# One residual-norm layer of a four-layer mix: its inverse root moved between engines, its scaling spread out, and two reorderings in the LSTM around it

## The chip, the cores and the metric

The kernel runs on one NeuronCore of a Trainium2 chip. Its engines work side by side, each with an instruction queue in order: TensorE (PE, matmuls; PEld are its weight loads), VectorE (DVE), ScalarE (ACT), GpSimd (POOL) and SyncE (SP), which here only issues DMAs. The metric is the time of one execution in microseconds (us), and lower is better. A profile shows one execution in detail; its span runs from the first instruction to the last, and the execution's own time is a little longer.

## The reference, cut to what matters

Four layers work on one tensor `x` of 128 x 64 x 256 (batch, nodes, features), each as a residual with a layer norm behind it. Layer 0 is the one that the change touches: a graph convolution, then for p = 1 to 4 an LSTM over windows of p neighbouring nodes, whose last hidden state replaces the last node of each window before the next p begins.

```python
def _L0_gnn_ref(x, adj, Wg0, bg0, Wg1, bg1, Wih, Whh, bih, bhh):
    h = relu(einsum('ts,bsh->bth', adj, x @ Wg0 + bg0))
    h = relu(einsum('ts,bsh->bth', adj, h @ Wg1 + bg1))
    for p in range(1, 5):
        nw = T // p
        wins = h[:, :nw * p, :].reshape(B * nw, p, Hd)
        last = _lstm_last(Wih[p-1], Whh[p-1], bih[p-1], bhh[p-1], wins)
        h = h.at[:, arange(nw) * p + (p - 1), :].set(last.reshape(B, nw, Hd))
    return h

def _layernorm(x, eps=1e-5):
    return (x - mean(x)) / sqrt(var(x) + eps)      # over the 256 features

x = _layernorm(x + _L0_gnn_ref(x, adj, ...))   # layer 0
x = _layernorm(x + _L1_gnn_ref(x, adj, ...))   # graph convolution, batch norms
x = _layernorm(x + _L2_gnn_ref(x, ..., adj))   # graph attention
x = _layernorm(x + _L3_gnn_ref(x, adj, ...))   # spectral: needs eigh(L_norm)
```

One LSTM step forms four gates i, f, g, o from `x_t @ Wih.T + h @ Whh.T + bias`, then `c = sig(f) * c + sig(i) * tanh(g)` and `h = sig(o) * tanh(c)`. Layer 3 needs the eigenvectors of a 64 x 64 matrix. They depend on `adj` alone, and the kernel works them out on VectorE during layer 0.

## The kernel before, in words

`x` lies in SBUF as the tile `X`: 64 tiles of 128 rows (two graphs of 64 nodes each) by 256 features. Layer 0 works on four groups of `TG` = 16 tiles (group 0 to 3). All matmuls are fp32.

**One group.** `convolve` (L1607) makes the group's hidden state `H` with features on the partitions. It is a generator, one `yield` after each small portion. `windows` (L1646) runs the LSTM of one p over the group. It splits the work into `parts`: four for p=1, two for p=2 and p=3 (one batch, that is, one graph of each tile pair, in each part), and a single one of both batches for p=4. A part has M columns: 512, or 336 for p=3. In a part, step `k` walks over the four gates `gt` (0 i, 1 f, 2 g, 3 o; f is skipped at k=0) and two feature halves `c`. One (gt, c) is one product tile in PSUM from the pool `pq`, which has four buffers: two input products (`inputs`, L1665 to L1670, reading `H` through `at`), for k>0 two recurrent ones (`recurrent`, L1672 to L1675, reading the last step's `lh`), and an eviction on ScalarE with sigmoid or tanh (L1696), which frees the buffer. For k>0 the two tiles of gate 0 are formed ahead, both inputs first and then the recurrent products (L1677 to L1682). VectorE forms the cell (L1703, L1706, L1708, L1709), ScalarE takes its tanh (L1710), VectorE multiplies by the output gate into `lh` (L1712) or, in the last step, into the places of `H` that end a window (L1717). So p=4 reads what p=3 has just written to `H`. The trace shows every fp32 matmul of the program as two records on PE, each with a weight load of its own.

**What is interleaved.** `pump` (L1699) lets the eigen solver (its pieces are lines 118 to 149 and about 800 to 880, tiny instructions on 64 partitions) go on by some instructions behind each eviction; VectorE's queue is shared by both. `side` (L1700) advances a generator by work done: `paced` (L1729) gives it `n` steps over a given amount of LSTM work. During p=3 and p=4 the side job is the next group's `convolve`. During p=1 and p=2 it is the previous group's `residual` (L1719): eight steps, each of which transposes two tiles of `H` back on PE (four transposes into the one buffer of the pool `pr`) and hands them to `ln.add`. Group 3's residual runs in the first pass of layer 1 (L1841).

**The norm.** `Norm.add` (L1273) adds the two tiles to `X` (L1279), takes the statistics of each (L1282, L1283) and after eight tiles calls `flush` (L1288). It calls `inv_sqrt` (L1251): on VectorE variance plus epsilon (L1257), on ScalarE a Sqrt (L1259), and on VectorE four more instructions that refine and invert it (L1260 to L1263). Then VectorE scales the eight tiles one behind the other (L1300). ScalarE's Sqrt needs another function table than sigmoid and tanh, which share one; a change of table is an instruction of its own, ACT_TABLE_LOAD. Layers 1 to 3 use `Norm` as well and are left as they are.

**What sets the order.** A scheduler may reorder instructions of an engine between the places where the program emits them, by dependences and pools; products marked with `keep_in_program_order` stay. SP's queue holds the weight loads of each p (`wi`, `wh`, 1 MB each), the inputs of the groups, and, from layer 1 on, copies of `X` to DRAM (`xd`).

## Time and profile before

| | us |
|---|---|
| three runs | 2254.89, 2255.51, 2256.37 |
| their median | 2255.51 |
| the profiled execution, its own time | 2254.81 |
| its span | 2253.0 |
| granted clock of PE, mean | 0.994 |
| POOL busy, of the span | 161.7 (7%) |
| idle of PE ahead of L1669 in layer 0 (77 to 1420 us) | 13.1 |
| its products there: L1669 (2010 records) and L1674 (1152 records), busy | 809.9 and 461.9 |
| evictions L1696 there (504), mean ns | 631 |

How to read it: "busy" is the time in which an engine has an instruction under way. A row of a timeline gives the start in us, the duration, the engine, the line, the operation, output and inputs by the program's names with their shapes, the number of instructions joined in it, and in brackets the idle time just before it and what ended that. A row of the waits gives who waited on which line, for whose result on which line, and the total, the number and the longest of these waits. "Slices" cut the span in 40 equal parts and give busy tenths in each. A row of the windows gives for a stretch of time its length, the busy time and the instructions of PE, PEld, DVE, ACT and POOL, and then the granted clock of PE, the share of time in which DMA is busy, and GB/s.

### The profile page before, as it was taken

How to read it: one execution, taken by the hardware profiler on the slowest of the kernel's cores; microseconds unless marked ns; L12 is line 12 of the kernel's file. 1: busy time of each engine (PE TensorE's matmuls, PEld its weight loads, DVE VectorE, ACT ScalarE, POOL GpSimd, SP SyncE). 2: the span in 40 equal slices, each digit the busy share in tenths (PEclk: the TensorE clock that was granted, in tenths of full speed). 3: DMA queues.
4: the chain of work that ended last, by engine and by line, in shares of the span. 5: the costliest groups of instructions: out<-in, count | busy, mean ns of one | idle time of the engine just before them, and what ended most of it. 6: DMA issues, size and time to landing. Idle time of an engine off the chain costs nothing. (4 is left out here: it accounts for less than half of the span.)

```text
span 2253.0 us, 29801 instructions
## 1 busy us (share of the span) xinstructions
PE 2197.9 (98%) x8746; PEld 1198.6 (53%) x8746; DVE 1808.5 (80%) x9217; ACT 952.3 (42%) x1746; POOL 161.7 (7%) x196
## 2 busy tenths in 40 slices
PE   8999999999999999999999999999999999999997
PEld 6445655445655445655444654554434333445987
DVE  5788887889888889888889998788947777657688
ACT  1432322433322343322343222434437876567675
POOL 0111111111000000000000000000000000100631
PEclk9999999999999999999999999999999999999999
DMA  7001010111010111010101000012210010221532
GB/s 233 22 19 38 1 39 1 38 38 57 1 38 1 38 38 57 1 38 1 38 38 56 1 19 19 20 54 98 74 54 24 29 42 24 77 74 43 151 90 80
DMA packets 44666, 101.53 MB, mean 45 GB/s; under 512 B 5297, under 2 KB 23857, under 8 KB 43217
## 3 DMA queue, kind: packets, MB, share of 16 engines
q1 hardware_dynamic: 38384, 84.64, 11.0%
q0 software_dynamic: 3984, 14.40, 2.3%
q8 instruction: 69, 1.13, 0.2%
q10 hardware_dynamic: 2128, 0.54, 0.1%
q14 instruction: 101, 0.82, 0.1%
HBM read 67.97 MB, written 31.59 MB: 44 GB/s over the span
## 5 line engine op out<-in xcount | busy, mean ns | idle before, releaser
L1669 PE MATMUL pq<-H,wi 128*128 128x512 f32 (+1 forms) x2016 | 812.6, 543 | 13.3 <-ACT gate L1696 7.0
L1696 ACT ACTIVATE gate<-pq,bl 128x512 f32<-128x512 f32 (+1 forms) x504 | 314.4, 631 | 610.6 <-PE pq L1674 497.8
L1669 PEld LDWEIGHTS pq<-H,wi 128*128 128x128 f32 x2016 | 377.2, 191 | 364.5 <-issue 281.1
L1674 PE MATMUL pq<-lh,wh 128*128 128x512 f32 (+1 forms) x1152 | 461.9, 528 | 0.9 <-DVE lh L1712 0.8
L1674 PEld LDWEIGHTS pq<-lh,wh 128*128 128x128 f32 x1152 | 218.1, 190 | 203.1 <-issue 144.2
L2097 DVE SCALAR_TENSOR_TENSOR xs<-xs 128x512 f32<-128x512 f32 x256 | 165.1, 685 | 70.1 <-ACT xs L2096 69.2
L1710 ACT ACTIVATE gate<-lc 128x512 f32<-128x512 f32 (+1 forms) x144 | 83.6, 580 | 276.4 <-DVE lc L1709 105.0
L2096 ACT COPY xs<-l 128x512 f32<-128x512 f32 x256 | 134.0, 596 | 53.9 <-PE l L2091 43.9
L2091 PE MATMUL l<-edge_s,xq 64*128 64x512 f32 x512 | 128.7, 616 | 0.4 <-ACT xs L2096 0.3
L2054 PE MATMUL m<-wqv,xT 128*128 128x512 f32 (+1 forms) x264 | 121.7, 597 | 2.8 <-DVE X L1279 1.9
L1913 PE MATMUL ps<-h,w 128*128 128x512 f32 x256 | 114.0, 603 | 3.2 <-ACT h L1907 3.2
L1298 ACT ACTIVATE X<-X,ln_sh,ln_rs 128x256 f32<-128x256 f32 x187 | 97.5, 592 | 40.7 <-DVE ln_sh L1294 31.2
L1860 PE MATMUL ps<-at,w 128*128 128x512 f32 x256 | 113.1, 593 | 0.0
L796 POOL PARTITION_ALL_REDUCE qQ<-qSG x62 | 73.5, 1186 | 512.6 <-DVE pc L134 291.1
L1282 DVE BATCH_NORM_STATS2 ln_st<-X 128x6 f32<-128x256 f32 x256 | 98.3, 414 | 1.5
L2054 PEld LDWEIGHTS m<-wqv,xT 128*128 128x128 f32 x264 | 46.4, 189 | 76.4 <-issue 36.1
L1913 PEld LDWEIGHTS ps<-h,w 128*128 128x128 f32 x256 | 48.6, 193 | 62.5 <-issue 53.2
L1860 PEld LDWEIGHTS ps<-at,w 128*128 128x128 f32 x256 | 47.2, 190 | 52.8 <-issue 51.9
L2091 PEld LDWEIGHTS l<-edge_s,xq 64*128 64x128 f32 x512 | 44.5, 186 | 56.9 <-issue 41.8
L1712 DVE TENSOR_TENSOR lh<-gate 128x512 f32<-128x512 f32 (+1 forms) x72 | 43.1, 602 | 33.7 <-ACT gate L1696 33.7
L130 DVE SCALAR_TENSOR_TENSOR CS<-GA,qE 64x1 f32<-64x1 f32 x294 | 61.7, 210 | 9.5
L130 DVE SCALAR_TENSOR_TENSOR GA<-qtg,CS,GA 64x1 f32<-64x1 f32 x294 | 61.6, 209 | 8.5
(611 smaller groups left out, 3277.1 us busy)
## 6 DMA issues: line engine op xcount, KB each, us to landing
wi<-in_WihT_dram SPq DMA_DIRECT2D x16, 1024.0 KB, 4.9
wh<-in_WhhT_dram SPq DMA_DIRECT2D x12, 1024.0 KB, 6.7
xd<-X SPq DMA_DIRECT2D x16, 512.0 KB, 2.6
X<-xd SPq DMA_DIRECT2D x16, 512.0 KB, 3.4
xv<-xv SPq DMA_DIRECT2D x32, 256.0 KB, 2.0
xr<-xv POOLq DMA_DIRECT2D x32, 256.0 KB, 3.0
X<-in_x_dram SPq DMA_DIRECT2D x15, 512.0 KB, 8.9
out_dram<-X SPq DMA_DIRECT2D x15, 512.0 KB, 2.9
```

Source lines behind the costliest of these rows:

```text
L130: self.nc.vector.scalar_tensor_tensor(o, a, s, b, op0, op1)
L1282: nc.vector.bn_stats(st, self.X[:, k, :])
L1298: nc.scalar.activation(x, x, AF.Identity, bias=sh[:, k : k + 1], scale=rs[:, k : k + 1])
L1669: te.matmul(ps, wi[:, kk, o * P : (o + 1) * P], at(kk, k), start=(kk == 0), stop=(k == 0 and kk == 1))
L1674: te.matmul(ahead[gt, c], wh[:, kk, o * P : (o + 1) * P], hst[:, kk, :M], start=False, stop=(kk == 1))
L1696: s.activation(gates[gt][:, c, :M], ps, AF.Tanh if gt == 2 else AF.Sigmoid, bias=bl[:, p - 1, o : o + 1])
L1860: te.matmul(ps, w1[:, k, c * P : (c + 1) * P], at[:, k, :], start=(k == 0), stop=(k == 1))
L1913: te.matmul(ys[c], w2[:, k, c * P : (c + 1) * P], h[:, k, :], start=(k == 2), stop=(k == 1))
L2054: te.matmul(pss[i][:, cols], xT[:, i, c, :], wqv[:, c, cols], start=(c == 0), stop=(c == 1))
L2091: mm = te.matmul(pl[:, b, :], xq[i][r, c * P : (c + 1) * P], GG[r, :], start=True, stop=True)
L2096: taken.setdefault(i, []).append(s.copy(x, pl[:, b, :]))
L2097: ready.append(v.scalar_tensor_tensor(x, x, 0.2, x, ALU.mult, ALU.max))
```

## The change

Four edits, all in layer 0:

1. `SpreadNorm` takes the place of `Norm`. After eight tiles it doesn't take the inverse root and scale them at once; it puts ten jobs on a list `late`: the first part of the root, the rest of it, and eight scalings of one tile each. `step(3)` does up to three of them. The root is computed on VectorE alone: a first value from the bits of the number (one multiply-add on them as integers), and three corrections, 12 instructions in all.
2. `residual` calls `ln.step(3)` ahead of each `ln.add`, and after its eight steps goes on until the list is empty. `paced` gives it `TG // 2 + 4` = 12 steps over the same amount of work instead of 8.
3. In p=4 at k=0 the four tiles of gates 0 and 2 are formed together by `by_batch`: first the columns of batch 0 of all four, then those of batch 1, in matmuls of 256 columns.
4. The cell's tanh is emitted behind the next eviction (`due`) instead of right where the cell is formed. In the built order the scheduler moves most of them back ahead of it.

```diff
+class SpreadNorm:
+    def add(self, t, src, n=1):
...
+        if len(self.todo) == self.n:
+            rs, h, q = (pool.tile([P, self.n], F32, tag=tag, name=tag) for tag in ("ln_rs", "ln_h", "ln_q"))
+            self.late += [lambda a=(rs, h, q, self.mv): self.first(*a), lambda a=(rs, h, q): self.more(*a)]
+            self.late += [lambda a=(t, k, self.mv, rs): self.scaled(*a) for k, t in enumerate(self.todo)]
+            self.todo = []
+
+    def step(self, n):
+        for _ in range(min(n, len(self.late))):
+            self.late.pop(0)()
+
+    def closer(self, y, h, q):
+        v = self.nc.vector
+        v.tensor_tensor(q, y, y, ALU.mult)
+        v.tensor_tensor(q, q, h, ALU.mult)
+
+    def first(self, y, h, q, mv):
+        v = self.nc.vector
+        v.tensor_scalar(h, mv[:, :, 1], 1e-5, 0.5, ALU.add, ALU.mult)
+        v.tensor_scalar(u(y), u(h), -0.5, float(0x5EF759DF), ALU.mult, ALU.add)
+        self.closer(y, h, q)
+        v.scalar_tensor_tensor(y, q, 1.5, y, ALU.subtract, ALU.mult)
+
+    def more(self, y, h, q):
+        v = self.nc.vector
+        self.closer(y, h, q)
+        v.scalar_tensor_tensor(y, q, 1.5, y, ALU.subtract, ALU.mult)
+        self.closer(y, h, q)
+        v.tensor_scalar(q, q, -1.0, 1.5, ALU.mult, ALU.add)
+        v.tensor_tensor(y, y, q, ALU.mult)
+
+    def scaled(self, t, k, mv, rs):
+        x = self.X[:, t, :]
+        self.nc.vector.tensor_scalar(x, x, mv[:, k, 0:1], rs[:, k : k + 1], ALU.subtract, ALU.mult)
...
-        ln = Norm(nc, hn, X, 8)
+        ln = SpreadNorm(nc, hn, X, 8)
...
-                    ahead = {}
+                    ahead, due = {}, []
...
+                    def by_batch(todo):
+                        for x in todo:
+                            ahead[x] = pq.tile([P, 512], F32, tag="pq", name="pq")[:, :M]
+                        h = M // 2
+                        for b in range(2):
+                            for gt, c in todo:
+                                o = gt * 2 + c
+                                for kk in range(2):
+                                    te.matmul(ahead[gt, c][:, b * h : (b + 1) * h], wi[:, kk, o * P : (o + 1) * P],
+                                              at(kk, k)[:, b], start=(kk == 0), stop=(kk == 1))
...
+                    elif p == 4:
+                        by_batch([(gt, c) for gt in (0, 2) for c in range(2)])
...
-                            if not k or gt:
+                            if (gt, c) not in ahead:
...
+                            while due:
+                                s.activation(*due.pop())
...
-                                s.activation(g[2], cs, AF.Tanh)
+                                due.append((g[2], cs, AF.Tanh))
...
+                ln.step(3)
                 ln.add(g * TG + j, ps, 2)
                 yield
+            while ln.late:
+                ln.step(3)
+                yield
...
-                side = paced(back, TG // 2, LOAD[1] + LOAD[2] - 4)
+                side = paced(back, TG // 2 + 4, LOAD[1] + LOAD[2] - 4)
```

More of the change, by code (lines that the diff above doesn't have):

```diff
@@ L1263, in inv_sqrt, with __init__ @@
     nc.vector.reciprocal(o, r)
+class SpreadNorm:
+    def __init__(self, nc, pool, X, n):
+        self.nc, self.pool, self.X, self.n = nc, pool, X, n
+        self.todo, self.late = [], []
+    def add(self, t, src, n=1):
+        v, pool = self.nc.vector, self.pool
+        if not self.todo:
+            self.mv = pool.tile([P, self.n, 2], F32, tag="ln_mv", name="ln_mv")
+        x = self.X[:, t : t + n, :].rearrange("p n d -> p (n d)")
+        v.tensor_tensor(x, src, x, ALU.add)
+        for k in range(t, t + n):
+            st = pool.tile([P, 6], F32, tag="ln_st", name="ln_st")
+            v.bn_stats(st, self.X[:, k, :])
+            v.bn_aggr(self.mv[:, len(self.todo), :], st)
+            self.todo.append(k)
+        if len(self.todo) == self.n:
[26 more added lines that the diff above has]
+        self.nc.vector.tensor_scalar(x, x, mv[:, k, 0:1], rs[:, k : k + 1], ALU.subtract, ALU.mult)
 class Norm:
```

## The prediction

> **What bounds the kernel now.** I read the busy shares first, then the slices, TensorE's waits in layer 0, and the timelines around each long wait.

> ```profile
> PE 2197.9 (98%) x8746; PEld 1198.6 (53%) x8746; DVE 1808.5 (80%) x9217; ACT 952.3 (42%) x1746; POOL 161.7 (7%) x196
> ...
> DVE  5788887889888889888889998788947777657688
> ```

> PE is busy 98% of the span, so time is won only where PE pauses or by less PE work. The change leaves the matmuls' work alone, so its worth lies in PE's pauses, and in layer 0 these are few. The second line shows who could make new ones: in the slices of layer 0 (3rd to 25th) VectorE is mostly busy eight or nine tenths. PE's two largest waits between 77 and 1420 us (total, times, longest; the others come to 2.6, of which 0.8 is L1674 waiting for VectorE's lh):

> ```profile
> PE pq L1669 <- ACT gate L1696: 7.0, 5, 2.1
> PE pq L1669 <- DVE H L1717: 5.9, 4, 2.3
> ```

> The first row is PE waiting for a free `pq` buffer, which a gate eviction on ScalarE must empty; the second is PE waiting for the H that p=3 writes and p=4 reads.

> A pause costs more than its idle. A record of 512 columns starts 0.429 us after the one before it and lasts 0.592, so a pause also loses 0.163 of overlap; and two records right after a pause take 1.13 where two elsewhere take 1.02 (rows of 298.64 and 300.05). I add 0.27 to each.

> **Part 1: the square roots leave ScalarE.** Today each flush of eight tiles puts a Sqrt on ScalarE. At the end of p=2 in group 2 (ScalarE, then PE):

> ```profile
> 880.18 0.63 ACT L1710 ACTIVATE gate<-lc 128x512 f32<-128x512 f32 x1 [3.84 <-DVE lc L1709]
> 880.83 1.28 ACT L1259 ACT_TABLE_LOAD   x1
> 882.13 0.21 ACT L1259 ACTIVATE is_s<-is_t 128x8 f32<-128x8 f32 x1
> 882.35 1.28 ACT L1696 ACT_TABLE_LOAD   x1
> 883.65 1.70 ACT L1696 ACTIVATE gate<-pq,bl 128x512 f32<-128x512 f32 x3
> ```

> ```profile
> 884.39 3.66 PE L1669 MATMUL pq<-H,wi 128*128 128x336 f32 x12 [1.86 <-ACT gate L1696]
> ```

> Two table loads and the root hold the evictions 2.80 us (1.28 + 0.21 + 1.28, and the starts between); PE pays 1.86. The same stands at 537.90 (0.88) and 1229.95 (2.12). Without them the evictions start when the tanh ends (880.81), before PE runs dry at 882.5. Gain: 0.88 + 1.86 + 2.12 + 3 x 0.27 = **5.67**. The first flush of each group (near 474, 821, 1165) loads tables too, but no PE pause follows: 0.

> The built order gains one table load, ahead of layer 1's root between its passes. There the last copy ends at 1558.93, so load and root would end near 1560.4, and VectorE reaches the reciprocal at about 1560.6. I take 0; uncovered, 1.28.

> **Part 2: p=4's first products by batch halves.** At the border from p=3 to p=4 PE waits for fresh H; group 0, then group 3:

> ```profile
> 298.64 1.13 PE L1669 MATMUL pq<-H,wi 128*128 128x512 f32 x2 [1.78 <-DVE H L1717]
> ...
> 300.05 1.02 PE L1669 MATMUL pq<-H,wi 128*128 128x512 f32 x2
> ```

> ```profile
> 1316.46 1.29 PE L1674 MATMUL pq<-lh,wh 128*128 128x336 f32 x4
> 1320.05 4.52 PE L1669 MATMUL pq<-H,wi 128*128 128x512 f32 x9 [2.30 <-DVE H L1717]
> ```

> The idles are 1.78, 1.51 (645.09), 0.35 (989.15), 2.30 and 0.13 (1322.16). With 5 x 0.27 they cost 2.05, 1.78, 0.62 and 2.96 by group. The p=3 window does batch 0 first, then batch 1, so batch 0's H is written long before. Now the batch-0 halves of four tiles go first: 8 program matmuls of 256 columns, two records each, 16 x 0.215 = 3.44 us that need no fresh H. That covers every wait, except that in group 3 the third tile's buffer is freed at 1319.38 (about 0.24 late), and the second batch-1 product needs the second H half, ready at 1322.16, which PE reaches near 1321.86 (0.30 + 0.27). Gain: 2.05 + 1.78 + 0.62 + 2.96 - 0.81 = **6.60**. The product's total is unchanged (2 x 0.215 against 0.429).

> It adds 8 matmuls per group, 64 weight loads in all, each about 0.19. In before the nearest rows are the products of 128 columns:

> ```profile
> 202.98 1.05 PE L1614 MATMUL ps<-bda,X 128*128 128x128 f32 x8
> ```

> Eight records in 1.05 us start about 0.11 apart, each with a load of 0.19; the loads do not show, so I take 0 (bounds 0 and 64 x 0.19 = 12.2). [...]

> **Part 3: the new VectorE work.** The inverse root by bits and three corrections is 12 small instructions per flush instead of 5, two flushes a group. Small dependent instructions start 0.20 apart; small independent ones 0.07:

> ```profile
> 533.99 0.17 DVE L1261 TENSOR_TENSOR is_r<-is_r,is_t 128x8 f32<-128x8 f32 x1
> 534.19 0.17 DVE L1262 SCALAR_TENSOR_TENSOR is_r<-is_r,is_s 128x8 f32<-128x8 f32 x1
> ...
> 534.63 2.67 DVE L1300 TENSOR_SCALAR X<-X,ln_mv,ln_rs 128x256 f32<-128x256 f32 x8
> ```

> ```profile
> 204.85 0.15 DVE L118 TENSOR_TENSOR ka<-qone,kk 64x1 f32<-64x1 f32 x1
> 204.92 0.15 DVE L118 TENSOR_TENSOR kq<-uc,kk 64x1 f32<-64x1 f32 x1
> ```

> So 7 x 0.20 = 1.4 per flush, 2.8 per group. The eight scalings start 0.323 apart; they keep their number, but come in threes.

> What matters is what comes ahead of the cell products that p=2's recurrent products wait for. With 12 steps instead of 8 over the same stretch, all eight adds now come before p=2's second half. By the built order the cell product there has ahead of it, beyond before: two adds with statistics (0.60 + 2 x 0.336 + 2 x 0.0985 = 1.47 each, 2.94), the second flush's 12 small ones (2.4), the first flush's extra 7 (1.4) and six scalings (1.94): 8.7 us, or 6.2 if the 19 small ones lie between other work at 0.07. VectorE waits, by the windows, for 4.8 us in 473 to 509, 2.7 in 820 to 853 and 3.2 in 1164 to 1198; filling these leaves 1.4 to 3.9, 3.5 to 6.0 and 3.0 to 5.5 for groups 1 to 3. The slack is today's gap between the end of lh and its product (0.06, 1.87, 0.99), plus 1.78 for two steps of transposes (0.89 each) that now run on PE ahead of that product: 1.84, 3.65, 2.77. New waits: 0 to 2.1, 0 to 2.35, 0.2 to 2.7; in all 0.2 to 7.2, to 8.0 with 0.27 for each. The pieces of the eigen solver lie between VectorE's instructions there, so the row of 0.07 is the nearer: I take **-1.5**. [...]

> Two pauses that late VectorE work makes in group 1 (507.34: 0.17; 509.56: 0.24) go, since an add with its statistics (from 502.50) moves away from just ahead of them: 0.41 + 2 x 0.27 = **0.95**. Group 3's p=4 gain of 2.15 is partly given back: VectorE has almost no idle from 1172 to 1369, and the eigen solver's product waits for it at 1380.88 (0.94) anyhow. I take **-1.5** of 2.15 (bounds 0 and 2.15).

> **Part 4: the cell's tanh.** Only about 21 of 144 tanh change places with an eviction in the built order; the others stood ahead or stay there. A place later is worth at most one eviction (0.57) on a chain with slack: 0. SP's `xd<-X` move ahead of the weight loads by some 20 us at 2.6 each, so no load comes later: 0. POOL's order is the same.

> **Sum:** 5.67 + 6.60 + 0.95 - 1.5 - 1.5 = 10.2 us. The profiled execution took 2254.81 (span 2253.0 and 1.81 around it), 0.70 under the median: 2244.6 for such an execution, **2245.3** as a median. Layer 1's first pass has VectorE waiting for some 15 us and the eigen work ends before it is needed, so the gain carries through.

> **Rivals.**
> - *New waits for lh take the place of the old ones.* Small instructions at full price: -8.0 instead of -1.5, no 0.95, and all of group 3's 2.15 lost: 5.67 + 6.60 - 8.0 - 2.15 = 2.1, median 2253.4. For it: VectorE at nine tenths; slack of 0.06. Against: the interleaving. 0.20.
> - *Slower: VectorE becomes the bound from group 1 on.* Its 2.8 more per group then stand on the path, 8.4, and the pauses' removal only lets PE wait elsewhere; only group 0's 2.05 is kept: +6.35, median 2261.9. It decides once 2.8 don't fit into VectorE's waits; in p=1 alone these are 12.1, 9.1 and 9.3 us (424 to 473, 770 to 820, 1115 to 1164). 0.06.
> - *The loads show.* 10.2 - 12.2: +2.0, median 2257.5. Against: the row of L1614. 0.04.
> - *More than forecast.* After the pause at 1229.95 the granted clock (the third column from the end) was 0.60:

> ```profile
> 1230.00:1234.00 4.00, 4.00 (x9) 2.52 (x10) 3.79 (x16) 1.93 (x5) 0.00 (x0) 0.60 0.68 275
> ```

>   PE lost 1.65 there. After 884.39 it did not, so I count 0. If it goes, with the pause at 1282.16 (1.98 + 0.27) and without new waits (1.5): 15.6, median 2239.9. 0.10.

> **Numbers.** The forecast has 0.60. The range reaches to the upper and the first rival, 2239.5 to 2253.5, and leaves the last two out. 0.2% (4.5 us, about what a measurement tells from no change) is 2251.0 to 2260.0: faster 0.60 + 0.10 = 0.70; within 0.20 + 0.04 = 0.24; slower 0.06.

> **What would show it.** Right: no ACT_TABLE_LOAD in layer 0, no wait at the end of p=2, p=4's first records of 256 columns without an idle ahead of them, their starts 0.215 apart. Wrong: L1674's wait for lh over 4 us (first rival), 256-column starts about 0.4 apart (loads), or PE's waits for VectorE in p=1 (slower).

## The result, and the profile after

| | before | changed |
|---|---|---|
| median of ten runs, us | 2255.51 (2254.44 to 2256.37) | 2248.25 (2245.57 to 2251.62) |
| ratio, 95% interval | | 0.997 [0.9961, 0.9978] |
| profiled execution: own time, span | 2254.81, 2253.0 | 2247.61, 2245.8 |

The change is 7.3 us faster; 10.2 were forecast. The changed kernel's runs also lie further apart, over 6 us instead of 2; the last section comes back to that. Its busy shares and VectorE's slices, from the page:

```profile
PE 2198.0 (98%) x8810; PEld 1212.1 (54%) x8810; DVE 1808.7 (81%) x9273; ACT 935.1 (42%) x1725; POOL 162.4 (7%) x196
...
DVE  5788887888898899888899998788847777656688
```

PE and VectorE have as much to do as before; the 64 additional records and 56 small instructions hardly show. TensorE's waits between 70 and 1420 us (total, times, longest):

```profile
PE eps L149 <- DVE dg L125: 2.7, 2, 1.8
PE pq L1725 <- ACT gate L1765: 1.3, 1, 1.3
PE pq L1741 <- DVE lh L1783: 0.4, 2, 0.2
PE ps L1696 <- DVE y L1690: 0.3, 1, 0.3
PE pq L1736 <- DVE H L1788: 0.3, 1, 0.3
```

(L1725 is the old L1669, L1741 the old L1674, L1736 the new half products, L1765 the eviction.) The 7.0 and 5.9 us that were the two largest waits are 1.3 and 0.3 now. Layer 0 has no ACT_TABLE_LOAD any more: ScalarE's last one ahead of it starts at 75.39, the next at 1549.21. The waits for lh, which the forecast feared, are 0.4. One row has grown: `eps L149`, a product of the eigen solver.

At the places of the edits 16.3 us were won, far more than forecast, and 9.5 were lost again further on. This table follows the same TensorE records through both profiles (time in before minus time in the changed kernel; another 0.62 lies ahead of layer 0's first recurrent product and belongs to no edit):

| from, to (time in before) | edit's place | TensorE earlier by |
|---|---|---|
| 276 to 314; 623 to 661; 968 to 1005; 1302 to 1334 | borders from p=3 to p=4 | 2.00; 1.74; 0.92; 2.11 |
| 384 to 568; 730 to 946; 1075 to 1256 | p=1, p=2 and the start of p=3, groups 1 to 3 | 1.65; 2.29; 4.19 |
| 1255 to 1283 | p=3 of group 3 | 1.38 |
| **1334 to 1391** | p=4 of group 3, product L149 | **-2.98** |
| 1415 to 1445 | start of layer 1 | -0.40 |
| **1490 to 1511** | layer 1's first pass, product L149 | **-3.76** |
| 1557 to 1588 | between layer 1's passes | -1.30 |
| 2116 to 2128 | layer 3, a copy `mc` on ScalarE | -1.07 |

The first three lines sum to 16.3, the others to -9.5; 0.2 more goes in small amounts. Two of the losing places, each around a product L149 (start, duration, engine, line, names, shapes, idle before):

```profile
1362.51 1.02 PE L1725 MATMUL pq<-H,wi 128*128 128x512 f32 x2
1365.37 0.30 PE L149 MATMUL eps<-dg,cst 64*64 64x32 f32 x2 [1.84 <-DVE dg L125]
1365.60 1.50 PE L1725 MATMUL pq<-H,wi 128*128 128x512 f32 x2
1367.04 0.42 PE L149 MATMUL eps<-qbd,sel 64*64 64x32 f32 x2
1367.39 3.08 PE L1741 MATMUL pq<-lh,wh 128*128 128x512 f32 x4
1370.30 1.88 PE L1725 MATMUL pq<-H,wi 128*128 128x512 f32 x4
```

```profile
1486.64 5.32 PE L1935 MATMUL ps<-at,w 128*128 128x512 f32 x12
1494.66 0.30 PE L149 MATMUL eps<-dg,cst 64*64 64x32 f32 x2 [2.70 <-DVE dg L125]
1494.89 2.79 PE L1935 MATMUL ps<-at,w 128*128 128x512 f32 x4
```

Four records of 512 columns take 1.88 us in the last line of the first fence, but 3.08 in the line above it and 2.79 in the second fence. They ran slowly right behind the pause. The windows there (length, busy times, then the granted clock, DMA share, GB/s):

```profile
1365.00:1371.00 6.00, 5.63 (x12) 2.52 (x13) 5.37 (x42) 1.12 (x2) 0.00 (x0) 0.72 0.01 1
1490.00:1500.00 10.00, 7.30 (x25) 3.78 (x24) 8.18 (x50) 2.88 (x6) 0.00 (x0) 0.83 0.27 107
```

The granted clock was 0.72 and 0.83. These two pauses cost their idle and, behind it, a slower clock: at 1365, of the 2.98 lost, 0.9 is more idle than in before and about 1.6 is clock (some 0.4 had gone ahead of it, with a wait for lh of 0.22 at 1345); at 1494 it is 2.2 and 1.6.

### The profile page after: what moved, and what is told of

The parts are those of the page before. It is cut to its first block, busy times and chain, and to the rows that moved or that the text cites. A ratio compares the mean times of both kernels' runs of the same rounds, so it can differ in the third digit from the quotient of the medians.

```text
span 2245.8 us, 29967 instructions
## 1 busy us (share of the span) xinstructions
PE 2198.0 (98%) x8810; PEld 1212.1 (54%) x8810; DVE 1808.7 (81%) x9273; ACT 935.1 (42%) x1725; POOL 162.4 (7%) x196
## 3 DMA queue, kind: packets, MB, share of 16 engines
q8 instruction: 70, 1.15, 0.2%
q10 hardware_dynamic: 2128, 0.54, 0.1%
## 5 line engine op out<-in xcount | busy, mean ns | idle before, releaser
L1725 PE MATMUL pq<-H,wi 128*128 128x512 f32 (+1 forms) x1952 | 781.0, 540 | 1.5 <-ACT gate L1765 1.3
L1765 ACT ACTIVATE gate<-pq,bl 128x512 f32<-128x512 f32 (+1 forms) x504 | 315.8, 632 | 617.8 <-PE pq L1741 503.4
L1725 PEld LDWEIGHTS pq<-H,wi 128*128 128x128 f32 x1952 | 365.5, 190 | 336.9 <-issue 270.3
L1741 PE MATMUL pq<-lh,wh 128*128 128x512 f32 (+1 forms) x1152 | 462.5, 529 | 0.5 <-DVE lh L1783 0.4
L1741 PEld LDWEIGHTS pq<-lh,wh 128*128 128x128 f32 x1152 | 218.8, 190 | 202.8 <-issue 144.1
L1768 ACT ACTIVATE gate<-lc 128x512 f32<-128x512 f32 (+1 forms) x144 | 83.6, 580 | 277.3 <-DVE lc L1780 111.7
L1338 DVE BATCH_NORM_STATS2 ln_st<-X 128x6 f32<-128x256 f32 x192 | 73.1, 416 | 1.2
```

What stands on the lines that cost most here:

```text
L1338: nc.vector.bn_stats(st, self.X[:, k, :])
L1725: te.matmul(ps, wi[:, kk, o * P : (o + 1) * P], at(kk, k), start=(kk == 0), stop=(k == 0 and kk == 1))
L1741: te.matmul(ahead[gt, c], wh[:, kk, o * P : (o + 1) * P], hst[:, kk, :M], start=False, stop=(kk == 1))
L1765: s.activation(gates[gt][:, c, :M], ps, AF.Tanh if gt == 2 else AF.Sigmoid, bias=bl[:, p - 1, o : o + 1])
```

## The experiments

Each kernel was compared with the kernel before on the same chip. The edit is against the kernel named. The median of before was 2254.6 beside the first four, 2255.4 beside the next four and 2255.3 beside the last, and 2255.51 beside the changed kernel. These medians differ by up to 0.9 and many of the intervals below overlap, so where two of these kernels lie one to three microseconds apart, the reading rests on their TensorE records more than on the medians.

| run | median, us (lowest to highest) | ratio to before, 95% |
|---|---|---|
| e_halves | 2254.19 (2251.62 to 2256.76) | 0.9997 [0.9988, 1.0006] |
| e_norm | 2250.40 (2247.47 to 2252.99) | 0.9979 [0.9969, 0.9989] |
| e_old_last | 2245.43 (2243.84 to 2246.52) | 0.9958 [0.9944, 0.9972] |
| e_root_twice | 2248.30 (2246.71 to 2254.09) | 0.9975 [0.9964, 0.9986] |
| e_no_tanh | 2248.89 (2244.85 to 2249.59) | 0.9967 [0.9955, 0.9979] |
| e_act_root | 2248.33 (2247.29 to 2250.79) | 0.9970 [0.9958, 0.9982] |
| e_steps8 | 2252.99 (2249.61 to 2255.08) | 0.9987 [0.9978, 0.9996] |
| e_pump | 2246.36 (2245.80 to 2247.89) | 0.9960 [0.9947, 0.9974] |
| e_block_last | 2249.76 (2247.66 to 2251.73) | 0.9975 [0.9965, 0.9984] |
| e_act_old_last | 2244.08 (2242.91 to 2244.93) | 0.9949 [0.9935, 0.9963] |
| e_pump_p1 | 2246.42 (2243.73 to 2247.43) | 0.9956 [0.9942, 0.9970] |
| e_awake | 2241.51 (2239.57 to 2244.14) | 0.9940 [0.9926, 0.9953] |

**The parts alone.** First the batch halves, added to before:

```diff
+                    elif p == 4:
+                        by_batch([(gt, c) for gt in (0, 2) for c in range(2)])
```

> The kernel before with the batch halves of p=4 alone. Theory A (a removed pause moves TensorE ahead by its length until TensorE meets a product of the eigen solver, L149, whose VectorE chain isn't faster): the four borders from p=3 to p=4 lose 2.0, 1.7, 0.6 and 2.2 us; group 3's share is given back at the two waits of L149, so 4.4 us are left, about 2251. Theory B (what the whole change gave back comes from the new VectorE work of the norm, not from TensorE being early): nothing is given back here, 6.6 us are left, about 2249. The starts of 256-column records are 0.215 apart in both.

By its profile TensorE gained 2.01, 1.74 and 0.66 at the first three borders. Behind the pause at the end of p=2 in group 3 it gained 1.7 more that belong to no edit: the slow clock that follows this pause in before did not come here. Then p=3 of group 3 took 3.3 back (waits for lh of 0.49 and 0.99, and a slow clock behind the pause of 1.94 at 1277), and the fourth border gained 3.1. At the end 2.9 were left in this profile, but its execution was among the quickest of eleven; by the medians almost nothing was left. Theory B is out. Theory A has the direction but not the size.

Then the norm's edits alone (before, with `SpreadNorm`, `ln.step(3)` and 12 steps):

> The kernel before with the norm's edits alone (root on VectorE, scaling spread, 12 steps); p=4's first products and the tanh as before. Theory A: the waits at the end of p=2 go (about 1.65, 2.3 and 4.2 us by group), TensorE is about 9 us ahead when it enters p=4 of group 3, and 3 to 4 us of that are given back at L149 and in a slower clock behind these waits: about 2250. Theory B: the give-back is that of the whole change, about 7 us, as it hangs on the norm alone: about 2253.5.

2250.4, as A said. The four waits for H at the borders stand as in before (1.77, 1.51, 0.32, 2.29), those at the end of p=2 are gone, and L149 near 1501 waits 3.13. Alone the two parts win 4.2 and 0.4, together 7.3; the intervals are too wide to tell whether that is more than their sum.

Taking the tanh's edit out of the changed kernel:

```diff
-                                due.append((g[2], cs, AF.Tanh))
+                                s.activation(g[2], cs, AF.Tanh)
```

> The changed kernel with the cell's tanh emitted where it was before. Theory A (only some 21 of 144 tanh change places, on a chain with slack): TensorE's starts stay within 0.3 us of the changed kernel's up to 1490 us, and the time is the same, about 2248 within the spread of these runs. Theory B (tanh behind the eviction frees product buffers sooner and so is part of the gain): pq waits for ScalarE's evictions come back at the ends of p=2 and in p=3, 1 us or more, about 2250.

Apart from 1.5 us that this execution was later from the start, its TensorE records follow the changed kernel's within 0.1 us up to 1345. The edit does nothing that can be measured.

**The small instructions.** The changed kernel with the root worked out twice per flush:

```diff
-            self.late += [lambda a=(rs, h, q, self.mv): self.first(*a), lambda a=(rs, h, q): self.more(*a)]
+            self.late += [lambda a=(rs, h, q, self.mv): (self.first(*a), self.more(*a[:3]), self.first(*a)),
+                          lambda a=(rs, h, q): self.more(*a)]
```

> The changed kernel with the inverse root worked out twice, 24 small VectorE instructions per flush instead of 12. Theory A (small instructions lie between other work, and p=2 has slack): L1741's waits for lh in p=2 stay below 2 us in all, and the time rises by 0 to 2.5 us, to about 2249.5. Theory B (each has its full price of 0.2 us on the path of the eigen solver and of the cell): 12 x 0.2 x 8 flushes = 19 us of VectorE work, of which at least 8 shows: 2256 or more.

TensorE's waits in layer 0 of that kernel (its lines are one higher):

```profile
PE eps L149 <- DVE dg L125: 2.7, 2, 1.8
PE pq L1726 <- ACT gate L1766: 1.2, 1, 1.2
PE pq L1742 <- DVE lh L1784: 0.8, 3, 0.4
```

Twelve more small instructions in each flush raise the waits for lh from 0.4 to 0.8, and the time stays (2248.30). In layer 0 the slack takes them: theory A.

**Table loads, or the place of the work?** The forecast put the pauses at the end of p=2 down to the two table loads. In this kernel the Sqrt returns to ScalarE, and all else stays as changed:

```diff
...
-            self.late += [lambda a=(rs, h, q, self.mv): self.first(*a), lambda a=(rs, h, q): self.more(*a)]
+            self.late += [lambda a=(rs, self.mv): inv_sqrt(self.nc, self.pool, a[0], a[1][:, :, 1], 1e-5), lambda: None]
```

> The changed kernel with the root worked out by ScalarE's Sqrt and the refinement of before, in one job of the list; scaling, steps and batch halves as changed. Theory A (the two table loads on ScalarE, 2.8 us, are what held the evictions at the end of p=2): TensorE waits for evictions return, some 1 to 2 us in each of groups 1 to 3, near the place of the second root, which now comes earlier in p=2: TensorE enters p=4 of group 3 about 4 us later than in the changed kernel; layer 1's wait near 1494 falls to 0.5 as in the run with the old norm there; in all about 2249. Theory B (it was the place of the root and of the eight scalings at the end of p=2 that mattered, not the engine): no such waits, about 2245, no worse than the changed kernel with the old norm in group 3.

Theory B for the waits at the end of p=2, but not for its time of 2245, since the wait for L149 in layer 1 stayed (2.82, see below). 2248.33 is the changed kernel's time, and in layer 0 its TensorE records lie within 0.65 us of the changed kernel's. ScalarE near the second root of group 2, and TensorE beside it:

```profile
835.33 1.28 ACT L1259 ACT_TABLE_LOAD   x1
838.87 0.21 ACT L1259 ACTIVATE is_s<-is_t 128x8 f32<-128x8 f32 x1 [2.25 <-DVE is_t L1257]
839.09 1.28 ACT L1765 ACT_TABLE_LOAD   x1
840.39 2.42 ACT L1765 ACTIVATE gate<-pq,bl 128x512 f32<-128x512 f32 x4
```

```profile
836.42 11.75 PE L1725 MATMUL pq<-H,wi 128*128 128x512 f32 x27
```

No eviction begins for 5.1 us, from 835.33 to 840.39, and TensorE runs on without a pause. At this place (k=0, records of 512 columns that start 0.43 us apart) each of the four buffers holds 4 x 0.43 = 1.72 us of products, 6.9 in all; at the start of p=3, where the loads stood in before (336 columns, 0.282 apart), it is 4 x 4 x 0.282 = 4.5. In before the evictions of group 2 also stood still for longer, 7.3 us from 876.35 to 883.65, and 3.84 of these were the tanh waiting for VectorE's cell: the two loads were only a part of that hold. The reverse test takes the spreading away and leaves the root on VectorE:

```diff
-                side = paced(back, TG // 2 + 4, LOAD[1] + LOAD[2] - 4)
+                side = paced(back, TG // 2, LOAD[1] + LOAD[2] - 4)
```

> The changed kernel with 8 steps of the residual over p=1 and p=2 instead of 12, so that the last jobs of the list (root and eight scalings of the second eight tiles) are emptied at the end of p=2. Theory A (the table loads made the waits there): the wait for evictions at the end of p=2 does not return; some 0.5 us of new waits for lh in p=3 of groups 2 and 3; about 2248.5. Theory B (the spreading made them go): VectorE's block of about 5 us at the end of p=2 holds the cell and so the evictions, 1 us or more in each group, about 2251.

Slower than the changed kernel by 4.7 (2252.99), and more than B said. TensorE, VectorE and ScalarE at the end of p=2 of group 2:

```profile
881.36 2.43 PE L1725 MATMUL pq<-H,wi 128*128 128x336 f32 x8
884.65 1.40 PE L1725 MATMUL pq<-H,wi 128*128 128x336 f32 x4 [0.86 <-ACT gate L1765]
886.49 1.78 PE L1741 MATMUL pq<-lh,wh 128*128 128x336 f32 x5 [0.44 <-DVE lh L1783]
```

```profile
878.73 1.38 DVE L1319 TENSOR_SCALAR X<-X,ln_mv,ln_rs 128x256 f32<-128x256 f32 x4
880.02 0.68 DVE L1788 TENSOR_TENSOR H<-gate 128x512 f32<-128x512 f32 x1
880.63 1.37 DVE L1319 TENSOR_SCALAR X<-X,ln_mv,ln_rs 128x256 f32<-128x256 f32 x4
...
883.16 0.49 DVE L1777 TENSOR_TENSOR lc<-gate 128x336 f32<-128x336 f32 x1
```

```profile
883.69 0.48 ACT L1768 ACTIVATE gate<-lc 128x336 f32<-128x336 f32 x1 [4.73 <-DVE lc L1777]
884.08 0.95 ACT L1765 ACTIVATE gate<-pq,bl 128x336 f32<-128x336 f32 x2
```

There is no table load here, and yet the wait for an eviction is back: the root's last instructions and eight scalings stand on VectorE ahead of the first cell of p=3 (L1777), the tanh (L1768) waits 4.73 us for that cell, and the next evictions stand behind the tanh. In group 3 the wait is for lh, 1.73 at 1228.5. By the records groups 2 and 3 lose 1.7 and 3.7 us there against the changed kernel. In group 1 the same block stands at the same place, and TensorE runs on without a pause:

```profile
533.59 2.02 DVE L1319 TENSOR_SCALAR X<-X,ln_mv,ln_rs 128x256 f32<-128x256 f32 x6
532.21 5.81 PE L1725 MATMUL pq<-H,wi 128*128 128x336 f32 x20
```

In before three table loads stood there (529.48, 533.92 and 535.86), and the pause of 0.88 went with them. So in groups 2 and 3 a block of work at this place makes the pause, on whichever engine it stands, while in group 1 the loads on ScalarE did. Taking the root off ScalarE was enough in group 1 alone, and with the 12 steps it was not needed in any group. The 12 steps do two things: the work comes earlier, and it comes in thirds. No run tells the two apart in these groups.

**Layer 1.** Group 3's norm runs there. With the norm of before for this group alone:

```diff
...
-                ln.add(g * TG + j, ps, 2)
+                (ln if g < NT // TG - 1 else last_ln).add(g * TG + j, ps, 2)
```

> The changed kernel, but group 3's residual (it runs in layer 1) takes the norm of before: root by ScalarE, eight scalings at once. Theory A: L149's wait near 1494 stays near 2.7 us, since TensorE is as early as in the changed kernel: 2248 within 1. Theory B: 14 small VectorE instructions and the scalings between the eigen solver's dependent ones made it: the wait falls to about 0.5, the slow clock behind it goes too, about 2244.5. A table load ahead of the root between the passes returns to the place it had before.

2245.43, 2.8 under the changed kernel:

```profile
1489.41 1.88 PE L1935 MATMUL ps<-at,w 128*128 128x512 f32 x4
1491.80 0.30 PE L149 MATMUL eps<-dg,cst 64*64 64x32 f32 x2 [0.51 <-DVE dg L125]
1492.03 1.56 PE L1935 MATMUL ps<-at,w 128*128 128x512 f32 x3
```

The wait is 0.51 instead of 2.70, and TensorE keeps 3.8 us. Theory B holds for this place. Which of the two differences does it, the small instructions or the spreading? With the VectorE root, but the list emptied at once for group 3:

```diff
+                if g == NT // TG - 1:
+                    ln.step(10)
```

> The changed kernel, root on VectorE throughout, but for group 3 (its residual runs in layer 1) the list is emptied at once where the eighth tile is added. Theory A (in layer 1 the scalings spread over later steps stand among the eigen solver's dependent instructions; the root's engine doesn't matter): L149's wait near 1494 falls from 2.7 to about 0.5 to 0.8, and the time to about 2245. Theory B (the 14 extra small instructions of the VectorE root made that wait): it stays above 2 us, about 2248.

The wait stayed (2.57), so theory A fell. But with the ScalarE root and the spreading (e_act_root) it was 2.82 as well: each alone is enough for a wait. The scheduler does not put the product at the same place in all of them, though. Counted from the end of layer 0, it is TensorE's 365th record in before, in the changed kernel and with the old norm, the 361st with the ScalarE root spread, the 369th with the VectorE root in a block, and the 379th with the root worked out twice. So the waits can't be compared as they stand. What can be is when VectorE starts `dg`, the result that the product waits for, counted from the same end of layer 0:

| norm of group 3 | start of `dg`, us |
|---|---|
| before; changed kernel with the old norm | 90.4; 90.8 |
| ScalarE root, spread (e_act_root) | 91.0 |
| VectorE root, spread (the changed kernel) | 93.0 |
| VectorE root, in a block (e_block_last) | 94.6 |
| VectorE root twice, spread (e_root_twice) | 96.3 |

The spreading alone makes `dg` 0.2 to 0.6 later. The 14 more small instructions of the VectorE root make it 2.0 later, and 24 more another 3.3, which is 0.14 for each in both cases. So the small instructions have the larger share, as theory B said. The spreading does lengthen the last steps of the chain, from the tile `num` of 16 columns to `dg`: seven scalings stand between them, and they take 6.7 us against 4.5 with the old norm. But with the ScalarE root that stretch also begins 2.1 sooner. A run with the product's place held was not made.

**Both together.** ScalarE root everywhere, spread in groups 0 to 2, the norm of before in group 3:

> The root on ScalarE everywhere, groups 0 to 2 spread as changed, group 3 with the norm of before. Theory A (the spreading alone removed the waits at the end of p=2): as fast as the changed kernel with the norm of before in group 3, 2245.4 within 1.5. Theory B (the VectorE root is part of the gain, the ScalarE root's table loads come back as pauses): 2248 or more.

2244.08: theory A. It has the lowest median of all versions without filler, though its interval overlaps that of e_old_last, and it needs no VectorE root at all.

**The eigen solver's share.** With `e_old_last` as the base, `pump`'s factors changed:

```diff
-... * PACE * (0.85 if p < 3 else 1.1))
+... * PACE * (0.95 if p < 3 else 1.0))
```

> The changed kernel with the norm of before for group 3's residual, and the eigen solver's share changed: 0.95 instead of 0.85 behind each eviction in p=1 and p=2, 1.0 instead of 1.1 in p=3 and p=4. Theory A (TensorE waits for the eigen solver's product near 1366 and for evictions near 1268 because VectorE lags behind in p=3 and p=4 of group 3): both waits (1.82 and 1.25) shrink by half or more, about 2243.5. Theory B (VectorE is full in group 3 whatever the split): the waits only move, 2245 within 1.5, or new lh waits in p=2 make it slower.

The waits near 1268 and 1366 went, but others came: 1.03 at 507, 0.56 at 852, 2.99 at 888 and, again for L149, 1.11 at 1391. At the end of layer 0 TensorE was 4.8 us behind the base; most of that came back between layer 1's passes, where the base's pause of 3.19 is 0.19 here. Theory B, with the median 0.9 above the base. Then with p=1 alone raised (`{1: 1.15, 2: 0.85}.get(p, 1.045)`):

> The changed kernel with the norm of before for group 3, and the eigen solver's share 1.15 in p=1 (0.85 before), 0.85 in p=2 as before, 1.045 in p=3 and p=4 (1.1 before), about the same in all. Theory A (VectorE has 9 to 12 us free per group in p=1 and none in p=3 and p=4 of group 3): no new waits in p=2; the waits near 1268 (1.25) and 1366 (1.82) shrink by 1 us or more in sum, about 2244. Theory B (what VectorE lags by doesn't depend on the split): 2245.4 within 0.7, or more.

2246.42, theory B by the time. The two waits did shrink as theory A said (that near 1268 is gone, that at 1365 is 1.12), but new ones stand in p=2 (0.94 at 512, 2.26 at 858), whose own share is unchanged. So VectorE's free time in p=1 is not free for this; which of its instructions made p=2's cells late was not followed up.

**The clock behind a pause.** Filler products between layer 1's passes, on the base `e_old_last`:

```diff
-    keep_awake(pp.tile([P, 512], F32, tag="ps", name="ps"), 2)
+    keep_awake(pp.tile([P, 512], F32, tag="ps", name="ps"), 5)
```

> The changed kernel with the norm of before for group 3, and five instead of two filler products on TensorE between layer 1's passes, where it pauses for 3.2 us until ScalarE's first eviction of the second pass. They add no result. Theory A (a pause of over about 1.8 us is followed by some us of half the clock): the pause shrinks to about 0.6, the granted clock behind it stays 1.0 instead of 0.5 over some 4 us, and TensorE is 1.6 to 2.8 us earlier from there on: about 2243.3. Theory B (the slow clock there comes from the load of the second pass itself, DMA and ScalarE): the clock falls all the same, 2245.4 within 0.7.

First the base's window behind its pause of 3.19 us (to 1550.42), then the filled kernel's TensorE and window:

```profile
1550.00:1556.00 6.00, 5.58 (x7) 2.49 (x8) 4.30 (x24) 5.41 (x8) 0.00 (x0) 0.50 0.53 183
```

```profile
1546.15 4.46 PE L1914 MATMUL ps<-Y,bdah 128*128 128x512 f32 x10
1551.23 9.28 PE L1988 MATMUL ps<-h,w 128*128 128x512 f32 x21 [0.62 <-ACT h L1982]
```

```profile
1551.00:1557.00 6.00, 5.77 (x14) 2.66 (x15) 4.47 (x24) 5.22 (x8) 0.00 (x0) 1.00 0.59 182
```

With the pause at 0.62 the granted clock stays 1.00 under the same DMA load, and 14 records run in 6 us where 7 did. The first product of the second pass starts as late as in the base, since it waits for ScalarE; the 3.0 us that TensorE wins here come in the 6 us behind it. Theory A, and the lowest median of all: 2241.51. One execution with the clock at 1.00 would not rule out theory B, as this fall does not come every time. But in the run without the tanh's edit the clock stayed 1.00 behind a pause of 3.31 at this place (1555 to 1561, DMA share 0.50), so the load of the second pass alone does not make it fall.

In the base the pause near 1366 was not followed by a slow clock:

```profile
1366.30 0.30 PE L149 MATMUL eps<-dg,cst 64*64 64x32 f32 x2 [1.82 <-DVE dg L125]
1366.53 1.12 PE L1725 MATMUL pq<-H,wi 128*128 128x512 f32 x2
1367.59 0.30 PE L149 MATMUL eps<-qbd,sel 64*64 64x32 f32 x2
1367.81 1.99 PE L1741 MATMUL pq<-lh,wh 128*128 128x512 f32 x4
```

The same four records take 1.99 here and 3.08 in the changed kernel, behind pauses of 1.82 and 1.84. The last section shows what tells them apart.

## Why the prediction was right, and where it was not

The time lies in the range and the forecast's direction is right; 7.3 us came of 10.2. Step by step:

- **Part 2, the batch halves: right.** 6.60 forecast, 2.00 + 1.74 + 0.92 + 2.11 = 6.77 found, with a wait of 0.3 left over in group 3. The half products ran without a gap:

```profile
294.95 1.29 PE L1741 MATMUL pq<-lh,wh 128*128 128x336 f32 x4
296.08 7.07 PE L1736 MATMUL pq<-H,wi 128*128 128x256 f32 x32
302.99 1.05 PE L1696 MATMUL ps<-bda,y 128*128 128x128 f32 x8
```

  32 records in 7.07 us, 0.216 apart by the median of all 124 intervals, with loads of 0.19 each: the loads don't show. The 12.2 us of the rival in which they show (64 loads of 0.19) did not come.
- **Part 1: the sum was right, the cause wrong.** 5.67 were to come from the table loads. Groups 1 to 3 did gain 1.65, 2.29 and 4.19 there, but a root on ScalarE, spread, gains the same, and a root on VectorE, not spread, does not in groups 2 and 3. The row of the profile (two loads between a tanh and the next eviction) was read rightly; that other work at this place would have done the same was not seen. In group 1 the forecast's cause holds, with three loads where it said "the same". Part 3 had priced the spreading as a cost alone, and it was the gain.
- **Group 3's 4.19** holds the 1.65 of slow clock that the forecast left in the rival "more than forecast", and 1.38 came behind it, where the pause at 1282 shrank from 1.98 to 1.26 and that at 1257 (0.54) went. That rival came true in part, and the give-back hid it.
- **Part 3's new waits: mis-sized.** -1.5 was taken; 0.4 us of waits came, and doubling the small instructions brought 0.4 more. It was not that the row of 0.07 always held: the twelve of group 1's second flush stand 0.20 apart (494.25 to 496.47), those of group 2's mostly 0.07 to 0.11 ahead of other work, and the wait for lh behind them is 0.17 in group 1 and none in group 2. The slack took either.
- **The 0.95 for two pauses in group 1** came about half: a wait of 0.17 remained at 507.34, and group 1 gained 1.65 where table loads and pauses together were to bring 2.10.
- **The step that failed** is the end of the sum, "-1.5 of 2.15" and "so the gain carries through". Not 1.5 but 9.5 was given back: 2.98 in p=4 of group 3, 3.76 in layer 1's first pass, 0.40 and 1.30 around the passes, and 1.07 in layer 3. Some 4.4 of this is slow clock (1.6, 1.6, and about 1.2 of the 1.30, where two stretches of 3.4 us at half the clock follow the pause, and one in before). The first two are waits for the eigen solver, which VectorE does not finish sooner because TensorE comes sooner, and which group 3's norm delayed in layer 1. That VectorE waits for 15 us there was no evidence: the chain L149 waits for is one of dependent instructions, and what is put ahead of them or between them delays it (`dg` by 2.2 against the old norm) though other stretches are idle.
- **The price of a pause** was too small. 0.27 on top of the idle was near for the pauses of 1.78 and 1.51 at the borders of groups 0 and 1, which gave 2.00 and 1.74. Behind those of 1.84 and 2.70 in the changed kernel about 1.6 of slow clock came each time, and the forecast counted the clock as 0.
- **Luck.** That the time lies in the range is in part luck. The places of the edits gave 16.3 where the sum had 5.67 + 6.60 + 0.95 - 1.5 = 11.7, and this surplus took up more than half of the 8.0 that were given back beyond the forecast.
- **Part 4 and the table load between the passes: right**, at 0 (the pause there is 3.31 after 3.19).

What stays open: the 1.07 in layer 3, a copy `mc` that starts later (TensorE waits 1.81 for it, 0.76 in before). The waits there differ from 0.8 to 2.5 between the profiles, and no run was made for it. Open as well is whether at the end of p=2 it helps more that the norm's work comes earlier or that it comes in thirds.

## What to carry to other kernels

When a pause ends at one engine's instruction, ask what would end it if that instruction cost nothing: here the place of the whole block was the cause in two groups of three, and bringing it forward in thirds cured the pause with the root on either engine. Before adding up removed pauses, follow the work to the next place where the engine meets a chain that doesn't get faster, and there put nothing between dependent instructions (here `dg` came 2.2 us later). Try each part alone and taken away, since a part can carry the gain that its neighbour was credited with.

## What the runs showed of the hardware that was not expected

Some of TensorE's pauses of 1.8 us or more were followed by a stretch at half the granted clock. The 14 profiles have 80 pauses of at least 0.8 between 75 and 1660 us. Behind none of the 41 below 1.8 did the clock fall. Of the 39 from 1.81 to 3.32, 27 were followed by a granted clock of 0.5 and 12 were not, among them three of 3.31 and 3.32. Behind the same pause of 1.8 near 1366 it fell in six kernels and not in three.

```profile
1362.80:1366.21 3.41, 1.57 (x6) 0.48 (x4) 3.24 (x24) 1.21 (x2) 0.00 (x0) 1.00 0.00 0
1366.21:1369.63 3.42, 3.42 (x7) 1.46 (x6) 2.79 (x21) 0.63 (x1) 0.00 (x0) 0.50 0.01 2
```

```profile
1361.89:1365.31 3.42, 2.60 (x7) 0.81 (x5) 3.18 (x19) 1.20 (x2) 0.00 (x0) 1.00 0.00 0
1365.31:1368.72 3.41, 2.42 (x8) 1.16 (x9) 3.35 (x23) 0.64 (x2) 0.00 (x0) 1.00 0.01 2
1368.72:1372.13 3.41, 3.41 (x9) 1.52 (x8) 3.34 (x28) 0.69 (x1) 0.00 (x0) 1.00 0.00 0
```

Of the windows of 3.41 us, all 17 with 2.07 us of pause or more were followed by a window at half the clock, 10 of the 20 with 1.72 to 2.01, and of the others, some 6,500, none that ran at the full clock itself. The pauses of 3.31 and 3.32 that got away were cut as well, with at most 2.01 in one window. A window at half the clock loses up to half its length, an estimate of 1.7 us; behind five of the pauses above 3.1 two ran so in a row (in the changed kernel from 1553.95 to 1560.77), and 2.9 to 3.1 were lost. How the grid lies to the kernel's first instruction differs between the profiles, over the whole 3.4 us: its first boundary comes 2.02 us behind that instruction in before and 0.88 in the changed kernel. So it looks like chance, for the kernel, which of its longer pauses are hit.

This also shows in the times. Put in the order of their times, the ten runs of the changed kernel are in the order of their mean granted clock too, from 0.994 (2245.57) to 0.991 (the three from 2251.41 on); 0.003 of 2250 us is 6.8, and the runs spread over 6.05. The changed kernel has three pauses of 1.8 or more (1.84, 2.70, 3.31) from 1365 us on, before only one (3.19): its others lie ahead of TensorE's waits for the eigen solver, which can take up a few microseconds. That this number makes the wider spread is argued, not shown: e_halves has only one such pause from 1365 us on, and its runs spread over 5.1.
